# Causal masks of the row-major scores: added by VectorE inside the maximum, one head at a time, in place of identity matmuls on TensorE

## The chip, the cores and the metric

The kernel runs on one core of a Trainium2 chip. The metric is the device time of one execution in microseconds, and the time of a kernel is the median of its runs. TensorE multiplies matrices into PSUM, VectorE, ScalarE and GpSimd work on tiles of 128 partitions, and SyncE issues most of the DMAs. The profile calls the engines PE (with PEld for its weight loads), DVE, ACT, POOL and SP.

## The reference

Two residual layers stand one behind the other: cross attention with 16 heads of 32 dimensions, and a mixture-of-experts feed-forward layer. The change lies in the attention. Cut to what matters:

```python
# x: (4, 1024, 512), ctx: (4, 1024, 512); 16 heads of hd = 32
xn = layernorm(x)
qh = heads(xn @ Wq.T); kh = heads(ctx @ Wk.T); vh = heads(ctx @ Wv.T + bv)
scores = einsum('bhsd,bhtd->bhst', qh, kh) / sqrt(hd)
mask = triu(ones((S, S), bool), k=0).at[0, 0].set(False)
scores = where(mask, -inf, scores)          # query s sees keys t < s; query 0 sees key 0
out = einsum('bhst,bhtd->bhsd', softmax(scores), vh)
x = x + merge(out) @ Wo.T + bo
x = x + ffn(layernorm(x))                   # 128 experts, each takes the best of 32 tokens
```

Masked scores must count neither in the maximum of a row nor in its sum.

## The kernel before

The attention is cut into 16 units: 4 batches times 4 groups of four heads (`R = 4`, 128 of the 512 hidden columns). Each unit computes its scores twice. First come the row-major scores (tile `sc`, queries on the partitions), from which only the maximum of every row is taken. Then come the key-major scores (tile `st`, keys on the partitions), from which a second small matmul takes the maxima away (line 473, `ones` by `mxT`), ScalarE takes the exponential (`pr`, line 481), GpSimd zeroes what the mask hides (line 484), and TensorE multiplies by the values (`av`, line 517). VectorE and GpSimd each add up half of the exponentials (`acc`, lines 500 to 504).

`score_piece(u, k)` makes one piece of row-major scores: 128 queries against at most 512 keys, four heads. A unit has twelve pieces. Query tiles 0 to 3 give one piece each (128, 256, 384 and 512 keys); tiles 4 to 7 give two each, a full one of 512 keys and one of 128, 256, 384 or 512. The last piece of each query tile ends on the diagonal (`diag`): 8 of 12. A piece fills two PSUM tiles of two banks, each with two heads. `key_block(u, k)` is its counterpart for `st`. Both draw from the same pool `ps_s` with three buffers, so that the four tiles of a step pass through three places: the second `st` tile of a step needs the first `sc` tile of that step to have been read by VectorE, and the next piece's first `sc` tile needs the second one.

In a diagonal piece the mask is one more matmul for each head: the identity in bf16 as weights, a 128x128 mask with 0 and -3.0e38 as the moving side, added onto the last 128 columns (lines 405 to 410). Then VectorE takes the maximum over both heads of a tile in one `tensor_reduce` with the sign turned (line 413, tile `nm`). `split_maxima` cuts the maxima into three bf16 parts (lines 426 to 433), which TensorE turns (line 439) for the subtraction in `key_block`.

The main loop runs unit by unit and step by step: the score piece `k` of unit `u + 1` beside the key block `k` of unit `u`. Between the two, and behind them, TensorE works on fill: projections `pk`, `pq`, `pv` of later units and output projections `po` of the batch before. The order on TensorE, VectorE, ScalarE and GpSimd is what the program writes out; nothing reorders it. Where fill goes is decided while the program is built, by a small plan: `now` is TensorE's clock in the plan, `dve` and `act` those of its readers, `scores_given` books what a piece costs TensorE and how long its reader takes, and `slot(..., until)` puts in fill until the plan says that the next two buffers are free. `beside(0.9)` puts small pieces of VectorE's own work in (layer norm, splits, the scaling `at` of finished rows) at a fixed rate. In `normalize`, `rd` holds the reciprocals of the row sums (line 549) and is written to DRAM by a DMA.

The names of the profile: `sc` line 401 the score matmuls, line 407 the mask matmuls, line 413 the maxima, `st` lines 467 and 473, `xnT` lines 239 and 240 the layer norm of the turned input.

Of the kernel before, what the change touches and what calls it, by code (L numbers as in the profile page):

```python
# [11 lines left out]
F32 = mybir.dt.float32  # L12
BF16 = mybir.dt.bfloat16
AF = mybir.ActivationFunctionType
ALU = mybir.AluOpType
AX = mybir.AxisListType
PSUM = bass.MemoryType.PSUM

P = 128
EPS = 1e-5  # L20
NEG = -3.0e38
# [16 lines left out]
def attention_phase(  # L38
# [11 lines left out]
    nc = tc.nc  # L50
    ident, ident16, mhalf = consts
# [4 lines left out]
    R = P // HD  # L56
    HS = 512
# [5 lines left out]
    LARGE, SMALL, TURN = 0.86, 0.11, 0.2  # L63
    now, dve, act, bank = [0.0], [0.0], [0.0], [0.0]
# [3 lines left out]
    def given(engine, cost):  # L68
        engine[0] = max(engine[0], now[0] + 0.2) + cost
        return engine[0]  # L70

    def scores_free():
        return max(read[0], read[1]) + 0.1

    def scores_given(work, engine, cost):
        now[0] = max(now[0], scores_free()) + work
        for _ in range(2):
            read.popleft()
            read.append(given(engine, cost))
# [4 lines left out]
    wpool = units.enter_context(tc.tile_pool(name="attn_w", bufs=1))  # L84
# [5 lines left out]
    spool = units.enter_context(tc.tile_pool(name="attn_small", bufs=2))  # L90
# [27 lines left out]
    def later(name, cost, work, front=False):  # L118
        pieces_left[name] = (cost, work)
        if front:  # L120
            aside.appendleft(name)
        else:
            aside.append(name)
# [237 lines left out]

    masks = []
    for name, base in (("first", 0), ("strict", -1)):
        m = wpool.tile([P, P], BF16, tag=f"mask_{name}", name=f"mask_{name}")
        nc.gpsimd.memset(m, 0.0)
        nc.gpsimd.affine_select(
            out=m, in_=m, compare_op=ALU.is_ge, fill=NEG, base=base,
            pattern=[[-(P + 2), P]], channel_multiplier=P + 1,
        )
        masks.append(m)  # L370
# [8 lines left out]
    for n in range(2):  # L379
        m = wpool.tile([P, 4, R, HD], BF16, tag=f"mxs{n}", name=f"mxs{n}")  # L380
# [7 lines left out]
    def score_piece(u, k):  # L388
        i, c0, n = pieces[k]
        kT, qT = ks[u], qs[u]  # L390
        half = i // 4
        if (u, half) not in nms:
            nms[u, half] = spool.tile([P, 2, 4, R], F32, tag=f"nm{half}", name=f"nm_{u}_{half}")
        nm = nms[u, half]
        scs = [
            ps_s.tile([P, 2, HS], F32, tag="sc", name=f"sc_{u}_{k}_{g}") for g in range(2)
        ]
        diag = c0 + n == (i + 1) * P
        for r in range(R):
            rr = ds(r * HD, HD)  # L400
            nc.tensor.matmul(  # L401
                scs[r // 2][:, r % 2, :n], lhsT=qT[rr, ts(i, P)], rhs=kT[rr, ds(c0, n)],
                start=True, stop=not diag,
            )
        if diag:
            for r in range(R):
                nc.tensor.matmul(  # L407
                    scs[r // 2][:, r % 2, ds(n - P, P)], lhsT=ident16,
                    rhs=masks[0 if i == 0 else 1], start=False, stop=True,
                )  # L410
        scores_given(LARGE * n / HS + (0.45 if diag else 0.1), dve, 0.15 + 2.1e-3 * n)
        for g in range(2):
            nc.vector.tensor_reduce(  # L413
                nm[:, c0 // HS, i % 4, ts(g, 2)], scs[g][:, :, :n], AX.X, ALU.max, negate=True
            )

    def split_maxima(u, half):

# [112 lines left out]
    def normalize(u, h):  # L531

        def multiply(rows):
            if h == 0:
                atTs[u] = opool.tile([P, S], F32, tag="atT", name=f"atT_{u}", bufs=7)
            nc.vector.tensor_tensor(atTs[u][:, ts(h, HS)], avs.pop((u, h)), rows, ALU.mult)

        pd = ps_m.tile([P, P], F32, tag="pm", name=f"pd_{u}_{h}")  # L540
        for g in range(4):
            for r in range(R):
                nc.tensor.matmul(  # L543
                    pd[ds(r * HD, HD), :], lhsT=pick[:, g, :],
                    rhs=accs[u, h, r // 2][:, r % 2, ts(g, P)],
                    start=(g == 0), stop=(g == 3),
                )
        yield 0.9, dve, 1.0
        rd = spool.tile([P, P], F32, tag="rd", name=f"rd_{u}_{h}")
        nc.vector.reciprocal(rd, pd)  # L550
        if (u, h) != (NU - 1, 1):
            n = 2 * u + h
            nc.sync.dma_start(inverse_dram[ts(n, P), :], rd)
            rows = qpool.tile([P, 4, P], F32, tag="inverse", name=f"inverse_{u}_{h}", bufs=1)
            for r in range(R):
                nc.sync.dma_start(
                    rows[ds(r * HD, HD), :, :],
                    inverse_dram[ds(n * P + r * HD, 4), :].partition_broadcast(HD),
                )
            later(("at", u, h), 0.8, lambda: multiply(rows.rearrange("p g q -> p (g q)")), front=True)  # L560
            later(("wait", u, h), 0.9, lambda: None, front=True)
            return

        spread = ppool.tile([P, 2, HS], F32, tag="pr", name="spread")[:, 0].rearrange(
            "p (g c) -> p g c", g=4
        )
        for g in range(4):
            nc.vector.tensor_copy(
                spread[:, g, :].rearrange("p (r m) -> p r m", m=HD),
                ident.rearrange("p (r m) -> p r m", m=HD)[:, :, g : g + 1].to_broadcast(  # L570
                    [P, R, HD]
                ),
            )
        yield None
        pb = ps_m.tile([P, 4, P], F32, tag="pm", name=f"pb_{u}_{h}")
        for g in range(4):
            nc.tensor.matmul(pb[:, g, :], lhsT=spread[:, g, :], rhs=rd, start=True, stop=True)
        yield 4 * 2 * SMALL, dve, 0.7
        multiply(pb.rearrange("p g q -> p (g q)"))
# [5 lines left out]
    fill, soon, done = deque(), deque(), set()  # L585
# [106 lines left out]
    for u in range(-1, NU):  # L692
# [28 lines left out]
        for k in range(STEPS):  # L721
            if u + 1 < NU:
                if k in (0, 4):
                    ensure(("q", u + 1, k // 4), ("k", u + 1, k // 4))
                score_piece(u + 1, k)
                if k == 4:
                    split_maxima(u + 1, 0)
                if k == STEPS - 1:
                    split_maxima(u + 1, 1)
# [5 lines left out]
            if u >= 0:  # L735
                h, j = blocks[k]
# [9 lines left out]
            if u >= 0:  # L746

                def add_first(u=u, k=k):
                    add_sums(u, k, 0, nc.vector)

                def weigh(u=u, k=k):
                    h, j = blocks[k]
                    ensure(("v", u, j // 4))
                    weigh_values(u, k)
                    if j == 4 * (h + 1) - 1:
                        if h == 0 and NC <= u and u % NC == NC - 1:
                            ensure(("o", u // NC - 1, NT - 1))
                        soon.append((now[0], normalize(u, h)))

                add_sums(u, k, 1, nc.gpsimd)  # L760
                sums.append(add_first)
                pending.append(weigh)
# [332 lines left out]
def xattn_ffn(ctx: ExitStack, tc, x, xT, ctxT, wqT, wkT, wvT, bv, woT, bo, ctrl, f1, biasT, f2, tie, out):  # L1095
# [23 lines left out]
    with tc.manual_schedule(engines=engines):  # L1119
        attention_phase(  # L1120
            tc, consts, x, xT, ctxT, wqT, wkT, wvT, bv, woT, bo, ctrl, tie,
            x2_dram, stats_dram, inverse_dram, routed,
        )
# [39 lines left out]
```

## Time and profile before

| | us |
|---|---|
| Median of 3 runs | 1498.17 |
| Lowest, highest run | 1489.71, 1499.57 |
| The profiled execution, its own time | 1487.66 |
| Its span, first to last instruction | 1485.9 |
| Score pieces (line 401), first to last start | 39.9 to 1090.5 |
| Mask matmuls (line 407), first to last start | 40.4 to 1091.7 |
| Mean granted TensorE clock | 0.972 |

The profile is of one execution. A row of a group gives busy time, the mean duration of one instruction, and the idle time of its engine just before it with what ended it. Durations of matmuls overlap, because they are pipelined; the distance from start to start is what a matmul takes of TensorE's time. The attention with score pieces lies between about 40 and 1092 us; what follows is the end of the attention, the routing and the feed-forward layer.

### The profile page before, as it was taken

To read this page: it belongs to the slowest core of one execution; us is meant where nothing else is said; L and a number is where in the kernel's file an instruction comes from. 1 tells how busy PE (TensorE), PEld (TensorE's weight loads), DVE (VectorE), ACT (ScalarE), POOL (GpSimd) and SP (SyncE) were. 2 spreads that over 40 slices of the span, in tenths; PEclk is the share of its full clock that TensorE was granted. 3 is DMA by queue.
4 is the path that set the end of the run, shared out by engine and by line. 5 is a ranking of instruction groups with operands and counts; after the bars stand their busy time and mean duration, and the time that the engine had idled before them with its cause. 6 is when DMAs were issued, how large, how long until landed. Compare 5 with 4: busy or idle time off the path is not lost.

```text
span 1485.9 us, 31726 instructions
## 1 busy us (share of the span) xinstructions
PE 1400.1 (94%) x13704; PEld 739.5 (50%) x13704; DVE 926.8 (62%) x1377; ACT 502.7 (34%) x785; POOL 486.4 (33%) x557
## 2 busy tenths in 40 slices
PE   6999999999899999999999999999997988968996
PEld 4344544354344534443434344444533547868886
DVE  3666777565657676666767755655754554756664
ACT  1033333423232233232323233232333124636662
POOL 1034334343334343435253443434366200000212
PEclk9999999999999999999999999999997996988999
DMA  8011201002231300012211100010113788652654
GB/s 298 21 50 32 76 24 66 20 1 59 38 111 36 96 29 19 10 52 47 72 60 50 33 11 10 10 38 19 38 47 122 268 273 241 191 193 79 207 181 143
DMA packets 96972, 125.25 MB, mean 84 GB/s; under 512 B 12992, under 2 KB 54336, under 8 KB 96704
## 3 DMA queue, kind: packets, MB, share of 16 engines
q1 hardware_dynamic: 94272, 114.84, 24.9%
q0 software_dynamic: 2560, 8.39, 1.9%
q8 instruction: 107, 1.75, 0.5%
q14 instruction: 33, 0.27, 0.1%
HBM read 91.78 MB, written 31.42 MB: 83 GB/s over the span
## 4 chain that ended last, share of the span: by engine, by line
PE 78%; issue 7%; DVE 5%; DMA 5%; POOL 2%; ACT 1%; SPq 0%; POOLq 0%; DVEq 0%; ACTq 0%
PE sc L401 12%; PE st L467 10%; PE av L517 8%; PE pq L288 8%; PE pk L274 8%; PE pv L307 8%; PE po L348 5%; PE pd L957 3%; PE sc L407 3%; DVE nm L413 2%; PE pi L976 2%; PE st L473 2%; PE po L808 2%; PE pl L845 2%; PE pd L543 2%
## 5 line engine op out<-in xcount | busy, mean ns | idle before, releaser
L413 DVE TENSOR_REDUCE nm<-sc 128x2 f32<-128x1024 f32 (+3 forms) x384 | 349.1, 951 | 265.3 <-PE sc L407 178.9
L481 ACT ACTIVATE pr<-st 128x1024 f32<-128x1024 f32 (+3 forms) x384 | 290.4, 808 | 583.9 <-PE st L473 557.6
L484 POOL TENSOR_SCALAR_AFFINE_SELECT pr<-pr 128x256 f32<-128x256 f32 x256 | 122.5, 488 | 383.0 <-ACT pr L481 380.9
L504 POOL TENSOR_TENSOR acc<-acc,pr 128x1024 f32<-128x1024 f32 (+3 forms) x128 | 209.2, 1634 | 93.3 <-ACT pr L481 85.6
L401 PE MATMUL sc<-kT,qT 32*128 32x512 f32 (+3 forms) x1536 | 206.3, 531 | 8.6 <-ACT pr L481 4.9
L467 PE MATMUL st<-qT,kT 32*128 32x512 f32 (+3 forms) x1536 | 191.1, 534 | 4.6 <-DVE nm L413 4.5
L517 PE MATMUL av<-pr,v 128*32 128x512 f32 (+3 forms) x1536 | 166.2, 501 | 8.0 <-POOL pr L484 4.3
L274 PE MATMUL pk<-ct,w_k 128*128 128x512 f32 x256 | 131.0, 629 | 10.0 <-DMA w_k<-in_wkT_dram 9.2
L307 PEld LDWEIGHTS pv<-w_v,ct 128*128 128x128 f32 x1024 | 119.5, 192 | 34.6 <-issue 25.6
L504 DVE TENSOR_TENSOR acc<-acc,pr 128x1024 f32<-128x1024 f32 (+3 forms) x128 | 126.5, 989 | 9.2 <-POOL pr L484 9.0
L467 PEld LDWEIGHTS st<-qT,kT 32*128 32x128 f32 x1536 | 68.6, 183 | 127.5 <-issue 99.8
L401 PEld LDWEIGHTS sc<-kT,qT 32*128 32x128 f32 x1536 | 74.4, 183 | 115.4 <-issue 50.6
L307 PE MATMUL pv<-w_v,ct 128*128 128x128 f32 x1024 | 131.4, 281 | 0.2 <-DMA w_v<-in_wvT_dram 0.2
L288 PE MATMUL pq<-xnT,w_q 128*128 128x512 f32 x256 | 127.3, 616 | 1.5 <-ACT xnT L194 1.5
L501 POOL TENSOR_TENSOR acc<-pr,pr 128x768 f32<-128x768 f32 (+1 forms) x32 | 66.8, 2086 | 161.4 <-ACT pr L481 161.4
L1074 POOL DMA_DIRECT2D out_dram<-xr x32 | 24.2, 757 | 259.2 <-DVE xr L1073 258.8
L348 PE MATMUL po<-w_o,atT 128*128 128x512 f32 x192 | 95.5, 616 | 0.0
L517 PEld LDWEIGHTS av<-pr,v 128*32 128x32 f32 x1536 | 32.1, 108 | 94.9 <-issue 67.2
L274 PEld LDWEIGHTS pk<-ct,w_k 128*128 128x128 f32 x256 | 43.9, 194 | 69.0 <-issue 54.2
L473 PE MATMUL st<-mxT,ones 32*128 32x512 bf16 (+3 forms) x768 | 74.6, 322 | 0.3 <-DVE mxT L444 0.3
L288 PEld LDWEIGHTS pq<-xnT,w_q 128*128 128x128 f32 x256 | 43.0, 189 | 52.9 <-issue 46.2
L1058 PE MATMUL pt<-ident,y 128*128 128x128 f32 x512 | 58.3, 277 | 5.3 <-DVE y L1033 4.6
(101 smaller groups left out, 1495.2 us busy)
## 6 DMA issues: line engine op xcount, KB each, us to landing
ct<-in_ctxT_dram SPq DMA_DIRECT2D x8, 1024.0 KB, 5.1
xt<-in_x_dram SPq DMA_DIRECT2D x8, 1024.0 KB, 5.8
xr<-in_x_dram SPq DMA_DIRECT2D x32, 256.0 KB, 2.7
xn_dram<-x SPq DMA_DIRECT2D x8, 1024.0 KB, 4.8
xn<-xn_dram SPq DMA_DIRECT2D x8, 1024.0 KB, 5.8
f<-in_f_dram SPq DMA_DIRECT2D x16, 512.0 KB, 4.1
xr<-x_dram SPq DMA_DIRECT2D x32, 256.0 KB, 4.1
f<-in_f_dram SPq DMA_DIRECT2D x32, 256.0 KB, 4.3
```

Of the source, the lines that this page charges most:

```text
L274: nc.tensor.matmul(pk, lhsT=weights["k"][:, c, ts(hc, P)], rhs=cts[b, half][:, c, :], start=(c == 0), stop=(c == NC - 1),)
L288: nc.tensor.matmul(pq, lhsT=weights["q"][:, c, ts(hc, P)], rhs=xnTs[b][:, c, ts(half, HS)], start=(c == 0), stop=(c == NC - 1),)
L307: nc.tensor.matmul(pv[:, t, :], lhsT=cts[b, half][:, c, ts(t, P)], rhs=weights["v"][:, c, ts(hc, P)], start=(c == 0), stop=(c == NC - 1),)
L348: nc.tensor.matmul(po, lhsT=atTs[b * NC + c][:, ts(t, P)], rhs=weights["o"][:, c, :], start=(c == 0), stop=(c == NC - 1),)
L401: nc.tensor.matmul(scs[r // 2][:, r % 2, :n], lhsT=qT[rr, ts(i, P)], rhs=kT[rr, ds(c0, n)], start=True, stop=not diag,)
L413: nc.vector.tensor_reduce(nm[:, c0 // HS, i % 4, ts(g, 2)], scs[g][:, :, :n], AX.X, ALU.max, negate=True)
L467: nc.tensor.matmul(scs[r // 2][:, r % 2, :n], lhsT=kT[rr, ts(j, P)], rhs=qT[rr, ds(h * HS + q0, n)], start=True, stop=False,)
L473: nc.tensor.matmul(scs[r // 2][:, r % 2, :n], lhsT=ones16[rr, :], rhs=mxT[rr, ds(q0, n)], start=False, stop=True,)
L481: nc.scalar.activation(pr[:, :, :n], scs[g][:, :, :n], AF.Exp)
L484: nc.gpsimd.affine_select(out=d, in_=d, compare_op=ALU.is_ge, fill=0.0, base=0 if j == 0 else -1, pattern=[[0, 2], [P + 1, P]], channel_mu ...
L504: engine.tensor_tensor(acc, acc, pr[:, :, :n], ALU.add)
L517: nc.tensor.matmul(avs[u, h][rr, q0:], lhsT=vs[u][:, j, rr], rhs=pr[r // 2][:, r % 2, : HS - q0], start=(j == 0), stop=(j == last),)
```

## The change

The mask matmuls are gone. In diagonal pieces the two `tensor_reduce` are replaced by four `tensor_tensor_reduce`, one for each head: each adds the mask to the scores, multiplies by -1, writes the result back in place into PSUM, and gathers the minimum of the result in one element of `nm` (the same number as the turned maximum). Since the instruction runs over all `n` columns of a piece, the mask of diagonal pieces other than the first gets 512 columns, zero but for its last 128, of which the last `n` are used. Full pieces keep the `tensor_reduce`. In the program, one `tensor_tensor_reduce` is two instructions on VectorE: the main one, and one that writes the gathered value to `nm`. The plan's figures follow: a diagonal piece costs TensorE 0.1 in place of 0.45 beside its scores, and VectorE 0.5 in place of 0.15 beside 2.1e-3 for each column of a tile. `rd` gets one buffer in place of two.

```diff
     for name, base in (("first", 0), ("strict", -1)):
-        m = wpool.tile([P, P], BF16, tag=f"mask_{name}", name=f"mask_{name}")
+        width = HS if base else P
+        m = wpool.tile([P, width], BF16, tag=f"mask_{name}", name=f"mask_{name}")
         nc.gpsimd.memset(m, 0.0)
         nc.gpsimd.affine_select(
-            out=m, in_=m, compare_op=ALU.is_ge, fill=NEG, base=base,
+            out=m[:, width - P :], in_=m[:, width - P :], compare_op=ALU.is_ge, fill=NEG, base=base,
             pattern=[[-(P + 2), P]], channel_multiplier=P + 1,
         )
...
-                start=True, stop=not diag,
-            )
-        if diag:
-            for r in range(R):
-                nc.tensor.matmul(
-                    scs[r // 2][:, r % 2, ds(n - P, P)], lhsT=ident16,
-                    rhs=masks[0 if i == 0 else 1], start=False, stop=True,
+                start=True, stop=True,
+            )
+        scores_given(LARGE * n / HS + 0.1, dve, (0.5 if diag else 0.15) + 2.1e-3 * n)
+        for g in range(2):
+            if not diag:
+                nc.vector.tensor_reduce(
+                    nm[:, c0 // HS, i % 4, ts(g, 2)], scs[g][:, :, :n], AX.X, ALU.max, negate=True
                 )
-        scores_given(LARGE * n / HS + (0.45 if diag else 0.1), dve, 0.15 + 2.1e-3 * n)
-        for g in range(2):
-            nc.vector.tensor_reduce(
-                nm[:, c0 // HS, i % 4, ts(g, 2)], scs[g][:, :, :n], AX.X, ALU.max, negate=True
-            )
+                continue
+            for r in range(2):
+                sc = scs[g][:, r, :n]
+                nc.vector.tensor_tensor_reduce(
+                    sc, sc, masks[0] if i == 0 else masks[1][:, HS - n :],
+                    -1.0, 3.0e38, ALU.add, ALU.min,
+                    nm[:, c0 // HS, i % 4, ds(2 * g + r, 1)],
+                )
...
-        rd = spool.tile([P, P], F32, tag="rd", name=f"rd_{u}_{h}")
+        rd = spool.tile([P, P], F32, tag="rd", name=f"rd_{u}_{h}", bufs=1)
```

## The prediction, made before the changed kernel ran

> **What bounds the kernel now.** I read the page's first part, then busy time by stage, then the rows of VectorE by shape, the waits, and the order of time around mask matmuls.
>
> ```profile
> PE 1400.1 (94%) x13704; PEld 739.5 (50%) x13704; DVE 926.8 (62%) x1377; ACT 502.7 (34%) x785; POOL 486.4 (33%) x557
> ```
> ```profile
> 40.00:104.00 64.00, 62.29 (x439) 27.07 (x440) 42.15 (x72) 13.80 (x20) 9.72 (x14) 1.00 0.06 17
> 104.00:1040.00 936.00, 920.61 (x7384) 413.22 (x7382) 614.09 (x879) 291.11 (x406) 374.26 (x394) 1.00 0.14 41
> ```
>
> In the second fence a line is one stretch: busy us of PE, PEld, DVE, ACT and POOL, then the clock. From 104 to 1040 us, where nearly all score pieces lie, TensorE idles 15.4 of 936 us at full clock: it is the bound. VectorE is busy 66%. The change takes work from the full engine and gives more of it to one with a third of its time free.
>
> ```profile
> L413 DVE TENSOR_REDUCE nm<-sc 128x2 f32<-128x1024 f32 x192 | 225.8, 1217 | 141.2 <-PE sc L401 85.6 <-PE sc L407 55.0
> L413 DVE TENSOR_REDUCE nm<-sc 128x2 f32<-128x768 f32 x64 | 58.3, 952 | 45.6 <-PE sc L407 45.5
> L413 DVE TENSOR_REDUCE nm<-sc 128x2 f32<-128x512 f32 x64 | 41.2, 685 | 38.3 <-PE sc L407 38.3
> L413 DVE TENSOR_REDUCE nm<-sc 128x2 f32<-128x256 f32 x64 | 23.9, 415 | 40.1 <-PE sc L407 40.1
> L354 DVE TENSOR_TENSOR xr<-po,xr 128x512 f32<-128x512 f32 x24 | 16.5, 686 | 21.7 <-PE po L348 13.1 <-POOL acc L500 6.3 <-issue 2.1
> L337 DVE BATCH_NORM_AGGREGATE moments<-row_stats 128x2 f32<-128x6 f32 x32 | 5.8, 182 | 1.1
> ```
>
> The four first rows are the maxima to be replaced in diagonal pieces: about 0.15 us and 1.04 ns for each element of a partition. The fifth is the nearest row to the new instruction (two inputs, one in PSUM): 512 elements in 0.686 us, the same slope and start. The sixth stands for a very small instruction.
>
> ```profile
> DVE nm L413 <- PE sc L407: 178.9, 105, 5.9
> ...
> DVE nm L413 <- PE sc L401: 85.6, 44, 3.9
> ...
> PEld st L467 <- DVE nm L413: 9.1, 8, 5.1
> ```
>
> Waits (total us, times, longest): of 192 pairs of maxima 149 found VectorE idle, 1.8 us on average. TensorE hardly waits for maxima.
>
> ```profile
> 536.85 1.14 PE L401 MATMUL sc<-kT,qT 32*128 32x512 f32 x8
> 537.92 1.98 PE L348 MATMUL po<-w_o,atT 128*128 128x512 f32 x4
> 539.84 0.71 PE L467 MATMUL st<-qT,kT 32*128 32x256 f32 x8
> ...
> 542.64 1.14 PE L401 MATMUL sc<-kT,qT 32*128 32x512 f32 x8
> 543.72 0.40 PE L407 MATMUL sc<-mask_strict,ident 128*128 128x128 bf16 x4
> 543.95 1.94 PE L274 MATMUL pk<-ct,w_k 128*128 128x512 f32 x4
> 545.82 0.50 PE L467 MATMUL st<-qT,kT 32*128 32x128 f32 x8
> ```
>
> The same piece without and with masks (start, duration, both us). Without: 1.07 us to the fill, whose four matmuls take 1.92 to the next start. With: 1.08 us to the masks, 0.23 more to the fill, whose four take 1.87.
>
> **The change part by part.** *Mask matmuls, removed.* 16 units x 8 diagonal pieces x 4 heads = 512 matmuls with their weight loads. From start to start a group of four costs 0.23 - 0.05 = about 0.19 us, so 128 x 0.19 = 25 us of TensorE. The chain of waits books 0.33 us for such a group (its share, 3%, is about 42 us): it counts pipeline ends that the next matmul would have had anyway. [...] I take the measured distance, 25 us, and keep 42 as the upper end. All of it lies on TensorE, thus on the path, unless a wait opens in its place.
>
> *Maxima of diagonal pieces, replaced.* 256 `tensor_reduce` go, 512 `tensor_tensor_reduce` come, each of two instructions. Two reductions in a row take 2 x 1.217 - 0.08 = 2.35 us at 512 keys (a pair in the timeline), so a piece of n keys costs 0.22 + 4.18e-3 n now. The main new instruction is 0.15 + 1.045e-3 n from the fifth row. The write-out is in no row: its lower bound is nothing, with the overlap of neighbours kept (-0.08 each); its upper is the smallest instruction, 0.18, and 0.04 for the wait that the second of each pair now has on VectorE itself (neighbours that wait are that far apart in the timeline). I take 0.08 in sum, since the write-out is a single element with no input stream. A diagonal piece then costs VectorE 0.92 + 4.18e-3 n, 0.70 us more than before, whatever n; bounds +0.07 and +1.27. For 128 pieces: +90 us (9 to 163). VectorE was busy 699 us between 40 and 1100; it would be 789 of about 1035, 76% (83% at the upper end). It writes PSUM here, which no row of this trace does; nothing excludes that this is slower, and the second rival prices it.
>
> [...]
>
> *What covers it.* The second `st` tile waits for the first `sc` tile. From the scores of two heads (0.53 us, at 512) TensorE has the other two heads (0.53), fill (1.0 to 1.4 us in the built order) and the first `st` tile (0.53): 2.1 us and more. Two new instructions need 2 x 0.77 = 1.5 us at 512, against 1.2 plus a wait on half the masks. So the margin hardly moves, and only a VectorE that comes late breaks it. In the built order the plan has moved fill to where it helps: between scores and key block of pieces 0, 3 and 7 0.2 us more on average, behind the key block 0.1 to 0.3 us less. Where is VectorE late? In the normalization of a new batch:
>
> ```profile
> 440.00:460.00 20.00, 19.58 (x144) 9.47 (x144) 17.92 (x19) 6.40 (x7) 9.63 (x6) 1.00 0.07 15
> ...
> 520.00:540.00 20.00, 20.00 (x104) 6.79 (x100) 17.28 (x17) 5.98 (x7) 10.75 (x9) 1.00 0.08 27
> ```
>
> Two more stretches are like this (720: 17.84, 800: 17.14). Each holds about 2.7 diagonal pieces, +1.9 us, which fills VectorE to 19 to 20 of 20 us. I book 1 us of TensorE waiting in each, 4 us, and 3 us for the rest: 7.
>
> *Waits added.* The second instruction of a pair waits for the first (counted). Queued behind it are the sums `acc` and the splits; `acc` frees `pr` buffers for ScalarE, but those are six, three steps deep. The reciprocal now also waits for the previous `rd` to have been stored; they come about 24 us apart (560.45 and 584.73) and the slowest store in the trace took 11.4: nothing.
>
> *Moved.* SP keeps its 286 DMAs; a few context loads, row stores and residual loads change places with neighbours, as do projection evictions on ACT and residual additions on POOL. One such collision is in the trace: at 370 us VectorE waited 7.6 us for `inverse` behind large loads, TensorE then 4.3 us for `nm`, and the clock was 0.50 from 374 to 380 us, about 3 us more. It can go or come once more: -8 to +8, booked as 0. The wider mask is a longer memset of GpSimd before 40 us, hidden behind the first loads: 0 (uncovered, below 1 us).
>
> *Sum.* 25 - 7 = 18 us less than 1487.66, so 1470. The median of the runs is 10.5 us above the profiled execution: 1480.
>
> **The rivals.** *First: nothing moves.* The mask matmuls were covering VectorE, and TensorE now waits in their place; or the write-out costs the upper bound. For it: the plan puts fill only up to the moment that buffers are free, and the steps with little fill (pieces 1 and 5, 0.2 us) have nothing to put in. Against: 1.8 us of idle VectorE before three of four pairs. At +1.27 us a piece the four full stretches overflow by about 2 us each and smaller ones follow: 20 to 30 us of waiting against 25. Time 1490 to 1505.
>
> *Second: VectorE becomes the bound, slower.* If adding in place in PSUM runs at half rate (2.09 ns an element), a diagonal piece costs 1.0 + 8.4e-3 n: 2.1, 3.2, 4.2 and 5.3 us for 0.75, 1.3, 1.8 and 2.35. That is 17 us a unit, 273 in all, and VectorE stands at 94%. [...] The first four steps of a unit then need 22 us of VectorE in 20.5 (+2 x 16), the stretches of normalization overflow by 3 (x 8), and the first pair of each of the four larger pieces misses the 2.1 us margin by 0.5 (x 64): 88 - 25 = 63 us slower, 1560. It decides from the point where a piece costs about 1.3 us more than before.
>
> **How the numbers follow.** A measurement of this kernel can tell about 1% (15 us) from no change. Forecast as worked out: 0.41; its own range 1464 to 1492, and a quarter of it within 1%. First rival: 0.23. VectorE as the bound, in a milder or full form (1514 to 1620): 0.36, that high because the engine that takes the work gets nearly four times what the other gives, and its two prices are unmeasured. Faster 0.32, same 0.32, slower 0.36. The range that leaves out the lowest 0.05 and the upper part of the second rival is 1464 to 1545.
>
> **What would show it.** Right: no mask rows; `sc` followed by fill at 1.07 us; the new rows near 0.69 us at 512 and 0.29 at 128, with write-outs below 0.1; VectorE near 790 us up to the end of the score pieces; TensorE's waits for `nm` under 20 us. Wrong: main rows above 1 us at 512; waits of `st` or `sc` for `nm` of 40 us or more; clock below 1.00 in several stretches of the attention.

## The result, and the profile after

| | before | after |
|---|---|---|
| Median of 4 runs, us | 1493.95 | 1510.19 |
| Lowest, highest run, us | 1489.71, 1499.57 | 1508.08, 1513.26 |
| Profiled execution, us | 1487.66 | 1508.76 |
| Last score matmul starts at, us (profiled execution) | 1091.0 | 1116.0 |

The ratio is 1.0106, with a 95% interval of 1.0062 to 1.0149: the kernel became 1.1% slower, 16 us where 18 fewer were forecast. What follows that last score matmul takes nearly the same time in both (394.9 and 391.1 us of the profiled executions).

First the page's busy times and the first two stretches of the attention (busy us of PE, PEld, DVE, ACT, POOL, then the clock):

```profile
PE 1398.2 (93%) x13192; PEld 719.4 (48%) x13192; DVE 989.9 (66%) x2145; ACT 503.0 (33%) x785; POOL 491.2 (33%) x557
```
```profile
40.00:104.00 64.00, 60.96 (x321) 26.50 (x324) 45.23 (x133) 9.35 (x15) 8.30 (x13) 0.89 0.02 8
104.00:1040.00 936.00, 901.62 (x6888) 391.43 (x6876) 657.36 (x1511) 289.62 (x401) 368.53 (x381) 0.98 0.14 42
```

512 matmuls and as many weight loads are gone, and VectorE has 768 instructions more. But TensorE idles 34.4 us of the 936 where it idled 15.4, and its clock, 1.00 in both stretches before, is now 0.89 and 0.98. The new rows of VectorE (line 415 of the changed kernel, busy us and mean ns; line 409 keeps the maxima of full pieces; READ_ACCUMULATOR is the write-out):

```profile
L415 DVE CUSTOM_DVE_ANT_0 sc<-sc,mask_strict 128x512 f32<-128x512 f32 x128 | 87.8, 706 | 35.3 <-PE sc L402 32.9
...
L415 DVE DVE_READ_ACCUMULATOR2_ANT nm<- 128x1 f32 x512 | 72.1, 141 | 0.0
...
L415 DVE CUSTOM_DVE_ANT_0 sc<-sc,mask_strict 128x128 f32<-128x128 f32 x64 | 18.3, 307 | 30.6 <-PE sc L402 29.6
```

The main one runs at 1.04 ns an element ((706 - 307) / 384), in place in PSUM too. What four heads of a 512-key piece take shows in the order of time, first the two reductions of before, then the new instructions:

```profile
544.04 2.35 DVE L413 TENSOR_REDUCE nm<-sc 128x2 f32<-128x1024 f32 x2 [1.31 <-PE sc L407]
```
```profile
552.97 0.70 DVE L415 CUSTOM_DVE_ANT_0 sc<-sc,mask_strict 128x512 f32<-128x512 f32 x1 [1.15 <-PE sc L402]
553.58 0.14 DVE L415 DVE_READ_ACCUMULATOR2_ANT nm<- 128x1 f32 x1
553.76 0.70 DVE L415 CUSTOM_DVE_ANT_0 sc<-sc,mask_strict 128x512 f32<-128x512 f32 x1
554.37 0.14 DVE L415 DVE_READ_ACCUMULATOR2_ANT nm<- 128x1 f32 x1
554.37 0.73 DVE L415 CUSTOM_DVE_ANT_0 sc<-sc,mask_strict 128x512 f32<-128x512 f32 x1
...
555.81 0.69 DVE L508 TENSOR_TENSOR acc<-acc,pr 128x512 f32<-128x512 f32 x1
```

A write-out begins while the main instruction still runs. The second head of a tile starts 0.04 us after the write-out of the first has ended (0.79 us from main to main); the head behind that starts together with the write-out (0.61). From 552.97 to 555.81 are 2.84 us, against 2.35 for two reductions. TensorE's waits for maxima between 40 and 1110 us (total, times, longest):

```profile
PEld st L471 <- DVE nm L409: 17.0, 6, 6.8
PEld sc L402 <- DVE nm L415: 16.0, 20, 1.2
PE st L471 <- DVE nm L409: 12.8, 4, 6.0
PEld st L471 <- DVE nm L415: 12.5, 17, 1.3
...
PEld sc L402 <- DVE nm L409: 6.3, 10, 1.3
...
PE sc L402 <- DVE nm L415: 5.6, 7, 1.0
```

Weight loads waited 51.8 us for `nm`, against 22.8 before. Of those 22.8 the prediction shows the 9.1 of `st`; the larger part was this one:

```profile
PEld sc L401 <- DVE nm L413: 13.7, 24, 1.3
```

It is the next piece's first `sc` tile that waits for the second one to be read. The weight load's wait and that of the matmul behind it overlap (at 674.40 us of after one stall ends both, 6.78 and 5.95 us), so the two kinds are not added.

To see where the time is, I cut the attention into stretches of 2 us, from 40 us to the last score piece, and summed TensorE's idle time and what a busy TensorE lost to a granted clock below 1. The rest is work, with the waits that modelled matmul ends cover:

| kernel | last score | idle | lost to the clock | rest |
|---|---|---|---|---|
| before | 1091.0 | 18.0 | 2.7 | 1030 |
| after | 1116.0 | 39.1 | 22.4 | 1015 |

The masks' removal is there: 15 us less in the rest. It is more than paid back by 21 us more of idling and 20 us more lost at half clock, so that the last score comes 25 us later. Before had one drop of the clock (374 to 381 us); after has eight, of 3.4 to 10 us each, from 60, 74, 115, 231, 381, 671, 702 and 805 us on. Two of them show the two kinds. The first, after short waits (start, duration):

```profile
58.38 0.70 PE L402 MATMUL sc<-kT,qT 32*128 32x256 f32 x4 [0.35 <-DVE nm L409]
59.51 3.33 PE L402 MATMUL sc<-kT,qT 32*128 32x512 f32 x8 [0.43 <-DVE nm L409]
62.77 3.78 PE L274 MATMUL pk<-ct,w_k 128*128 128x512 f32 x4
...
67.73 1.98 PE L274 MATMUL pk<-ct,w_k 128*128 128x512 f32 x4
```

Two gaps of 0.4 us, then a clock of 0.50 from 60.49 to 67.31 us: the four `pk` matmuls that take 1.98 at 67.73 take 3.78 at 62.77. The second kind is the stall that before had once, at 370 us, and after has twice. SP's queue around 655 us, first before, then after:

```profile
642.60 0.38 SPq L216 DMA_DIRECT2D stats_dram<-ln_both  x1
653.76 0.34 SPq L235 DMA_DIRECT2D both<-stats_dram  x1
654.15 1.83 SPq L553 DMA_DIRECT2D inverse_dram<-rd  x1
658.06 1.71 SPq L556 DMA_DIRECT2D inverse<-inverse_dram  x4
```
```profile
654.35 0.38 SPq L216 DMA_DIRECT2D stats_dram<-ln_both  x1
654.78 0.58 SPq L557 DMA_DIRECT2D inverse_dram<-rd  x1
666.04 0.34 SPq L235 DMA_DIRECT2D both<-stats_dram  x1
666.77 2.06 SPq L560 DMA_DIRECT2D inverse<-inverse_dram  x4
```
```profile
671.73 0.69 DVE L542 TENSOR_TENSOR atT<-raw,inverse 128x512 f32<-128x512 f32 x1 [8.91 <-DMA inverse<-inverse_dram]
...
673.16 2.32 DVE L409 TENSOR_REDUCE nm<-sc 128x2 f32<-128x1024 f32 x2
...
674.40 1.22 PE L471 MATMUL st<-qT,kT 32*128 32x512 f32 x2 [5.95 <-DVE nm L409]
```

Before, the reciprocals `rd` were issued after the statistics of a layer norm had landed, and were on their way back 3.9 us later. After, they are issued 0.4 us behind the statistics and return only 12 us later. VectorE waits 8.91 us at `at` with the maxima queued behind it; TensorE waits 5.95 us for those, and its clock is 0.50 from 671.48 to 681.72 us. Nothing of this touches a mask.

### The profile page after: what moved, and what is told of

Its sections match the earlier page's. It is cut to its first block, busy times and chain, and to the rows that moved or that the text cites. A ratio compares the mean times of both kernels' runs of the same rounds, so it can differ in the third digit from the quotient of the medians.

```text
span 1507.1 us, 31644 instructions
## 1 busy us (share of the span) xinstructions
PE 1398.2 (93%) x13192; PEld 719.4 (48%) x13192; DVE 989.9 (66%) x2145; ACT 503.0 (33%) x785; POOL 491.2 (33%) x557
## 4 chain that ended last, share of the span: by engine, by line
PE 72%; DVE 10%; issue 8%; DMA 5%; POOL 2%; ACT 2%; SPq 0%; POOLq 0%; DVEq 0%; ACTq 0%
PE sc L402 10%; PE st L471 10%; PE pk L274 8%; PE pq L288 8%; PE av L521 8%; PE pv L307 8%; PE po L348 5%; PE pd L961 3%; PE pi L980 2%; DVE sc L415 2%; PE po L812 2%; PE st L477 2%; DMA inverse_dram<-rd 2%; PE pl L849 2%; PE pd L547 1%
## 5 line engine op out<-in xcount | busy, mean ns | idle before, releaser
L415 DVE CUSTOM_DVE_ANT_0 sc<-sc,mask_strict 128x256 f32<-128x256 f32 (+3 forms) x448 | 230.6, 535 | 154.6 <-PE sc L402 146.7
L508 POOL TENSOR_TENSOR acc<-acc,pr 128x1024 f32<-128x1024 f32 (+3 forms) x128 | 213.0, 1664 | 89.0 <-ACT pr L485 70.6
L471 PE MATMUL st<-qT,kT 32*128 32x512 f32 (+3 forms) x1536 | 208.4, 542 | 15.6 <-DVE nm L409 12.8
L409 DVE TENSOR_REDUCE nm<-sc 128x2 f32<-128x1024 f32 x128 | 150.5, 1216 | 59.1 <-PE sc L402 58.0
L274 PE MATMUL pk<-ct,w_k 128*128 128x512 f32 x256 | 135.0, 649 | 9.6 <-DMA w_k<-in_wkT_dram 9.2
L471 PEld LDWEIGHTS st<-qT,kT 32*128 32x128 f32 x1536 | 71.8, 185 | 150.6 <-issue 93.4
L508 DVE TENSOR_TENSOR acc<-acc,pr 128x1024 f32<-128x1024 f32 (+3 forms) x128 | 130.2, 1017 | 11.7 <-POOL pr L488 11.5
L307 PE MATMUL pv<-w_v,ct 128*128 128x128 f32 x1024 | 134.9, 286 | 1.4 <-ACT qT L293 1.4
L348 PE MATMUL po<-w_o,atT 128*128 128x512 f32 x192 | 98.6, 632 | 0.0
L477 PE MATMUL st<-mxT,ones 32*128 32x512 bf16 (+3 forms) x768 | 79.6, 326 | 0.0
```

The costliest lines, as they stand in the source:

```text
L274: nc.tensor.matmul(pk, lhsT=weights["k"][:, c, ts(hc, P)], rhs=cts[b, half][:, c, :], start=(c == 0), stop=(c == NC - 1),)
L307: nc.tensor.matmul(pv[:, t, :], lhsT=cts[b, half][:, c, ts(t, P)], rhs=weights["v"][:, c, ts(hc, P)], start=(c == 0), stop=(c == NC - 1),)
L348: nc.tensor.matmul(po, lhsT=atTs[b * NC + c][:, ts(t, P)], rhs=weights["o"][:, c, :], start=(c == 0), stop=(c == NC - 1),)
L409: nc.vector.tensor_reduce(nm[:, c0 // HS, i % 4, ts(g, 2)], scs[g][:, :, :n], AX.X, ALU.max, negate=True)
L415: nc.vector.tensor_tensor_reduce(sc, sc, masks[0] if i == 0 else masks[1][:, HS - n :], -1.0, 3.0e38, ALU.add, ALU.min, nm[:, c0 // HS, i ...
L471: nc.tensor.matmul(scs[r // 2][:, r % 2, :n], lhsT=kT[rr, ts(j, P)], rhs=qT[rr, ds(h * HS + q0, n)], start=True, stop=False,)
```

## The experiments

A time is the median of 4 to 20 runs; a ratio is to before on the same chip (there 1494.6 to 1495.6), with its 95% interval.

**e1: the change, but with the plan's figures of before.**

```diff
-        scores_given(LARGE * n / HS + 0.1, dve, (0.5 if diag else 0.15) + 2.1e-3 * n)
+        scores_given(LARGE * n / HS + (0.45 if diag else 0.1), dve, 0.15 + 2.1e-3 * n)
```

> The changed kernel with the plan's two figures of before (0.45 and 0.15 for a diagonal piece), so that fill, projections and DMAs stand in the order of before; only the masks' place differs. Theory A (VectorE comes late: the new instructions are longer and TensorE stands, whatever the order): 1505 to 1515 us, waits of TensorE for nm 20 us or more, several drops of the granted clock. Theory B (the new figures made a worse order, above all the row statistics' store ahead of the store of rd on SP at 650 us, which holds the multiplications of at): 1470 to 1485 us, no stall of 6 us near 650 to 690, waits for nm under 10 us.

1492.61 us, 0.9988 (0.9970 to 1.0007): no difference from before. The plan's figures alone are worth the 17.6 us between this run and after.

**e2: the reverse, before with the new figures.**

```diff
-        scores_given(LARGE * n / HS + (0.45 if diag else 0.1), dve, 0.15 + 2.1e-3 * n)
+        scores_given(LARGE * n / HS + 0.1, dve, (0.5 if diag else 0.15) + 2.1e-3 * n)
```

> The kernel before, masks by TensorE and one reduction for two heads, with the plan's new figures (0.1 and 0.5). Theory A: the order is harmless where VectorE is quick, 1488 to 1500 us. Theory B: most of the loss is here already, 1505 to 1525 us, with the stall at 650 to 690 us in the trace.

1515.55 us, 1.0130 (1.0091 to 1.0170). With the masks on TensorE the new figures cost 20 us; they need none of the change's instructions to do so.

**e3: no mask at all in the maxima, figures of before.** The row-major scores give nothing but the row's maximum, and softmax may subtract any number near it: here the maximum over the hidden scores of the piece too, which this kernel's maxima no longer leave out. All pieces use `tensor_reduce`; the mask matmuls and the new instructions are both gone, and what hides scores from the sums (line 484 of the kernel before) stays. The edit, against before:

```diff
-                start=True, stop=not diag,
-            )
-        if diag:
-            for r in range(R):
-                nc.tensor.matmul(
-                    scs[r // 2][:, r % 2, ds(n - P, P)], lhsT=ident16,
-                    rhs=masks[0 if i == 0 else 1], start=False, stop=True,
-                )
+                start=True, stop=True,
+            )
```

> The kernel before without its mask matmuls and with nothing in their place: the maximum of a row is taken over the hidden scores of its piece too, which softmax allows as long as nothing overflows; the order of before. It measures what 512 mask matmuls are worth when VectorE is given no more work. Both theories: 25 us less than before (0.19 us a piece), 1465 to 1475; if the chain's 0.33 us is right, 1450 to 1460; if masks only filled TensorE's waits, 1485 to 1495.

1467.67 us, 0.9815 (0.9773 to 0.9857). Against before, it is what the mask matmuls are worth: 27.4 us (21 to 34 by the interval). Against e1, it is what VectorE's new instructions cost in the same order of work: 24.9 us. (e1 also has `rd` with one buffer and the wider mask; in its trace no `rd` waits for a store.) The weight loads' waits for maxima, first of e1, then of e3:

```profile
PEld sc L402 <- DVE nm L415: 19.8, 29, 1.2
...
PEld st L471 <- DVE nm L415: 14.7, 20, 1.1
...
PEld st L471 <- DVE nm L409: 13.1, 10, 6.3
...
PEld sc L402 <- DVE nm L409: 6.0, 8, 1.3
```
```profile
PEld st L461 <- DVE nm L407: 14.1, 19, 5.7
PEld sc L401 <- DVE nm L407: 11.5, 20, 1.3
```

53.6 us against 25.6. Of e1's, 34.5 us are 49 waits for the new instruction, 0.7 us each, none long enough to stand out. `sc` and `st` share the growth: `sc` waits 25.8 us in place of 11.5, `st` 27.8 in place of 14.1.

**e4: the masks on both engines, each adding half, figures of before.**

The changed kernel with the mask matmuls of before put back beside the new instruction. The edit, against after (the plan's line is that of e1):

```diff
-NEG = -3.0e38
+NEG = -1.5e38
...
-                start=True, stop=True,
-            )
...
+                start=True, stop=not diag,
+            )
+        if diag:
+            for r in range(R):
+                nc.tensor.matmul(
+                    scs[r // 2][:, r % 2, ds(n - P, P)], lhsT=ident16,
+                    rhs=masks[0] if i == 0 else masks[1][:, HS - P :], start=False, stop=True,
+                )
```

> Masks added twice, by TensorE and by VectorE (each with half of the number), in the order of before: VectorE's new work alone, with nothing taken from TensorE. Theory A: 1515 to 1535 us, as TensorE keeps its masks and waits on top. Theory B: VectorE's extra 0.5 us a piece lies in idle time, 1490 to 1505 us.

1511.71 us, 1.0109 (1.0076 to 1.0142). Each engine has its price beside the other: VectorE's part costs 16.6 us over before, TensorE's 19.1 over e1. That is 8.3 us less for each than without the other (24.9 and 27.4), as much as the intervals of the four medians leave open (about 8 us, an estimate from the three ratios). That the two hide a part of each other is possible, and not shown.

The table of the attention, for these:

| kernel | last score | idle | lost to the clock | rest |
|---|---|---|---|---|
| e3, no masks | 1072.7 | 20.7 | 4.3 | 1008 |
| e1, VectorE, old figures | 1095.9 | 29.7 | 7.0 | 1019 |
| after, VectorE, new figures | 1116.0 | 39.1 | 22.4 | 1015 |
| e2, TensorE, new figures | 1123.5 | 30.2 | 19.9 | 1033 |
| e4, both, old figures | 1121.3 | 27.2 | 11.5 | 1043 |

With mask matmuls the rest is 1030 to 1043, without them 1008 to 1019. The new figures bring 15 us more at half clock with VectorE's masks (e1 to after) and 17 with TensorE's (before to e2).

Each row is one profiled execution, and these scatter: e1's is the second fastest of 20 (1487.64 us at a mean clock of 0.973; the others reach 1501.29 at 0.959), e2's the slowest of 5. Over all runs, the span times what the mean granted clock lacks to 1 averages 46 to 48 us for before, 50 for e1, 49 for e5, 52 for e6, 55 for e11, 59 for e2 and 62 for after. From e1 to after that is 12 of 17.6 us, from before to e2 14 of 20.5: the clock is about two thirds of it.

**e5, e6: one of the two figures at a time.** The change with only TensorE's new figure, 0.1 (e5), and with only VectorE's, 0.5 (e6).

```diff
+        scores_given(LARGE * n / HS + 0.1, dve, 0.15 + 2.1e-3 * n)
```
```diff
+        scores_given(LARGE * n / HS + (0.45 if diag else 0.1), dve, (0.5 if diag else 0.15) + 2.1e-3 * n)
```

> The changed kernel with only TensorE's new figure in the plan (0.1 for a diagonal piece; VectorE's stays 0.15). If the poor order comes from the TensorE figure, 1505 to 1515 us; if from the VectorE figure, 1485 to 1497 us with a mean clock of 0.97; if the two figures only shuffle an order that is as good as chance makes it, anything between, and the clock's drops in places of their own.

> The changed kernel with only VectorE's new figure in the plan (0.5 for a diagonal piece; TensorE's stays 0.45). If the poor order comes from the VectorE figure, 1505 to 1515 us; if from TensorE's, 1485 to 1497 us.

1491.84 us, 0.9981 (0.9955 to 1.0006), and 1492.10 us, 0.9978 (0.9960 to 0.9996). With VectorE's masks neither figure is slow by itself; both together are. Both of these have the second stall as well. In e6:

```profile
645.07 0.38 SPq L216 DMA_DIRECT2D stats_dram<-ln_both  x1
645.51 0.57 SPq L557 DMA_DIRECT2D inverse_dram<-rd  x1
...
658.15 1.85 SPq L560 DMA_DIRECT2D inverse<-inverse_dram  x4
...
662.85 0.69 DVE L542 TENSOR_TENSOR atT<-raw,inverse 128x512 f32<-128x512 f32 x1 [9.31 <-DMA inverse<-inverse_dram]
```

So the stall that after has over before does not make the difference by itself (e5 has it too, with `rd` issued 0.4 us behind the statistics at 650.57 us).

**e7, e8: the load of the statistics put later.** I took the stall to be SP's order: `both` waits on SP for its statistics, and `inverse` behind it. In e7 (after) and e8 (e3) the load is handed to the list of small pieces, 0.9 us of the plan later, with a small memset of VectorE on its tile.

```diff
-        spread_stats(0)
+        later(("hold", b), 0.9, lambda: None)
+        later(("spread", b), 0.0, lambda: spread_stats(0))
```

> The changed kernel with one thing moved: the load of both (the row statistics spread over the partitions) waits on SP until VectorE has come one step further, by a write of four columns, so that the loads of inverse no longer stand behind a load that waits for the store of the statistics. If those two stalls (near 380 and 670 us: 4.9 and 6.0 us of TensorE's waiting and some 4 us each at half clock) are a large part of the loss, 1488 to 1497 us and no wait for inverse above 4 us; if the loss lies in VectorE's lateness, 1503 to 1512.

> No masks in the maxima (as in the run without masks) and the same later load of both. The stall near 368 us in that run was 4.9 us of waiting and about 4 us at half clock: 1456 to 1463 us if it goes, 1466 to 1470 if another wait takes its place.

1514.81 us, 1.0124 (1.0070 to 1.0178), and 1466.27 us, 0.9807 (0.9754 to 0.9860). Nothing was won: that reading fell. SP's queue in e7, and the store's line in its chain of waits:

```profile
366.18 0.38 SPq L216 DMA_DIRECT2D stats_dram<-ln_both  x1
366.61 0.99 SPq L560 DMA_DIRECT2D inverse_dram<-rd  x1
378.37 1.71 SPq L563 DMA_DIRECT2D inverse<-inverse_dram  x4
```
```profile
366.61 11.74 DMA inverse_dram<-rd
```

`both` is out of the way, and the store of `rd` still takes 11.74 us. It is late behind the store of the statistics, issued 0.4 us before it.

**e9, e10: that store on GpSimd's queue instead,** in after and in e3.

```diff
-                nc.sync.dma_start(
+                nc.gpsimd.dma_start(
                     stats_dram[2 * b + half].rearrange("s (i p) -> p s i", p=P), mv
```

> The changed kernel with the store of the row statistics (1024 elements of 4 bytes) issued by GpSimd, on its own queue, in place of SP's. In the traces the store of rd that SP issued 0.4 us behind it took 11.4 to 11.9 us to land, VectorE waited 8 to 9 us for inverse and TensorE 5 to 6 us for nm, at 380 and 670 us. If the queue is what holds rd, both stalls and their half clock go: 1488 to 1497 us, longest wait for inverse under 4 us. If the 16 engines hold it whatever the queue, 1505 to 1515 us.

> No masks in the maxima, the order of before, and the statistics' store on GpSimd's queue: the same test where only one such stall (at 367 us) is left. If the queue holds rd, 1456 to 1462 us; if not, 1465 to 1470; if GpSimd's own issue of 1024 pieces delays its sums, 1470 or more.

1520.53 us, 1.0161 (1.0127 to 1.0195), and 1470.90 us, 0.9829 (0.9793 to 0.9866). Not faster either. From the chain of waits of e9:

```profile
363.24 10.36 DMA stats_dram<-ln_both
...
373.99 4.76 DMA inverse_dram<-rd
```

The store of the statistics takes 10.36 us on this queue too. That of `rd` no longer lies behind it and takes 4.76; but SP issues it only at 373.99, behind the load of `both`, which had waited for those statistics. With e7 one of the two obstacles was removed and the other held; with e9 the reverse. Both at once I did not try, so what the stall costs in full stays open.

**e11: the change with the figure that was measured,** 0.35 for VectorE. 2.84 us for the four heads at 512 keys are 1.42 a tile, and 0.35 + 2.1e-3 x 512 = 1.43.

```diff
-        scores_given(LARGE * n / HS + 0.1, dve, (0.5 if diag else 0.15) + 2.1e-3 * n)
+        scores_given(LARGE * n / HS + 0.1, dve, (0.35 if diag else 0.15) + 2.1e-3 * n)
```

> The changed kernel with VectorE's figure in the plan as measured (a tile of a diagonal piece takes 1.42 us at 512 keys and 0.63 at 128: 0.35 and 2.1e-3 a column) in place of 0.5; TensorE's stays 0.1. If the loss is a plan that has VectorE too slow, 1485 to 1495 us; if any order is as good as another, up to 1512.

1498.87 us, 1.0005 (0.9982 to 1.0029): 11 us better than after, and no better than e1, e5 and e6, whose figures are wrong.

**e12: e3 with a plan that knows that no masks are left** (0.1 and 0.15).

```diff
-        scores_given(LARGE * n / HS + (0.45 if diag else 0.1), dve, 0.15 + 2.1e-3 * n)
+        scores_given(LARGE * n / HS + 0.1, dve, 0.15 + 2.1e-3 * n)
```

> No masks in the maxima, and the plan told so (0.1 and 0.15 for every piece). If a plan that knows its costs gives the better order, 1455 to 1464 us; if orders differ by chance, 1460 to 1485.

1476.62 us, 0.9866 (0.9836 to 0.9897): 9 us slower than e3, whose plan still books 0.35 us for masks that are not there. A truer plan is not a better order. And here TensorE's figure alone does cost something, as it did not in e5.

## Why the prediction was wrong, step by step

The sum was 25 - 7 + 0 = 18 us faster. By the medians, the same terms are: 27.4 faster without mask matmuls (before to e3), 24.9 slower with VectorE's additions (e3 to e1), 17.6 slower with the new order (e1 to after): 15.1 slower.

Two terms failed, by nearly the same amount: what moved (0 booked, 17.6 measured) and the waits (7 booked, 24.9 measured). The waits alone would have left about no change, as in e1; only with the moved work does the kernel become slower.

- *Moved, "-8 to +8, booked as 0": the step that turned the sign.* The new order costs 17.6 us with the masks on VectorE and 20.5 with them on TensorE. I had looked for one stall that could come or go once more. It did come once more, but e5 and e6 have it too and are not slow. Most of it is clock: in the profiles after's last score comes 20 us behind e1's, made up of 15 us at half clock (22.4 - 7.0), 9 more of idling and 5 less in the rest; over all runs it is 12 us of clock. The forecast named the clock as a sign of error and gave it no price. It held that the plan had moved fill to where it helps; the waits of weight loads for `nm` are 51.8 us in the new order and 53.6 in the old one.
- *Waits, 7 us: the other step that failed.* They measured 24.9 (in the profiles 9 of idling, 3 at half clock, 11 in the rest). I priced places where VectorE has no time left, four stretches of 20 us, and reckoned the margin for the second `st` tile alone. The next piece's `sc` also waits, and did so before (13.7 us): about half of the growth lies there. The waits came in small pieces everywhere: VectorE's longer chain from scores to maxima is on TensorE's path at many steps although VectorE idles over a quarter of the time (751 busy of 1070 us from 40 on, in after). "The margin hardly moves" was wrong: 0.5 us more for four heads was enough to double the waits in front of weight loads (25.6 us in e3, 53.6 in e1).
- *Mask matmuls, 25 us: right.* 27.4 measured (128 x 0.19 is 24.3, which was rounded up). Distance from start to start was the better measure; the chain's 42 us were too high.
- *Price of a diagonal piece on VectorE, 0.70 us: somewhat high.* It is 0.49 at 512 keys (2.84 against 2.35). The main row was right (706 ns for 0.69 us), the write-out overlaps more than I had assumed: at 553.58 us it begins 0.61 us after the start of a main one of 0.70. Up to the end of the score pieces VectorE was busy 62 us more than before (761 between 40 and 1120, 699 between 40 and 1100), which is 128 x 0.49; 90 more were forecast.
- *Eight instructions of VectorE for two, on an engine with time to spare:* they cost 24.9 us (e3 to e1). No run separates their number from the 0.49 us that they add to each piece.
- *`rd` with one buffer and the wider mask, 0:* they were not tried alone, and are part of the 24.9. Nothing speaks against it: `rd` never waits for a store in the traces of e1 and after, and the first scores start at 40.9 us in e1 and 40.6 in e3.
- *Second rival, in-place PSUM at half rate:* refuted, 1.04 ns an element.
- *First rival, "the mask matmuls were covering VectorE, and TensorE now waits in their place", 1490 to 1505:* this is what the change does when the order stays. e1 has 1492.61. Its waits of 20 to 30 us against 25 are what was measured, though the way there was not: the write-out is cheap, not dear, and the overflow of "about 2 us each" is 0.6 to 1.4 us by the prediction's own figures (2.7 x 1.27 on top of 17.1 to 17.9 of 20). It was outweighed by idle VectorE "before three of four pairs", an average that says nothing on the steps where the maximum is late.

Not settled is why both figures together make a poor order where each alone does not. The orders of e1, e5, e6 and e11 lie within 7 us of each other, with 7 to 18 us lost to the clock; after and e2 lose 20 to 22. That is a difference of degree, and a reason beyond where the gaps happen to fall, which the last section shows, was not found.

## What to carry to other kernels

A cost figure in a plan is part of a change: it reorders everything behind it. Here the new figures cost 17.6 us, where the new instructions in the old order made no difference (e1). So run the new instructions in the old order and the old instructions in the new one before judging either. Work moved to an engine with idle time was not free here: TensorE awaits its result, and it cost 24.9 us (e3 to e1). So count the steps at which the result is awaited, not the idle share of the engine that takes the work. And ask first whether the work is needed: the maximum needs no mask, and leaving it out (e3 and e8, 1466 to 1468 us, 1.9% below before) beats both ways of applying it, as long as hidden scores don't tower over the visible ones so far that the exponentials vanish.

## What was not expected of the hardware

The granted clock fell to 0.50 after gaps of TensorE far shorter than the stalls: two of 0.4 us at 58 to 60 us, one of 1.29 us at 114, one of 0.67 at 229, and it stayed there for 3.4 to 10 us. After's eight drops cost 22.4 us, 2.8 each on average. The two drops at the stalls (waits of 4.93 and 5.95 us) are 6.0 of the 22.4 us; before each of the other six no gap was longer than 1.68 us.

Not every short gap does it, and gaps that did it at one place did not at another. In after's trace all eight drops between 40 and 1090 us begin on one grid with steps of 3.41 us and last one to three steps: they begin at 60.49, 74.14 and 115.10 us and so on, the second 4 steps and the third 16 steps behind the first. The drops that stretches of 2 us show in the traces of e1 to e9 and e11 lie on such a grid too; e5's begin at 61.36, 75.00, 112.56, 378.80 and 668.92 us, the later ones 4, 15, 93 and 178 steps behind the first. After has the same two gaps of TensorE, 1.68 and 0.69 us, at 505 and at 801 us; here are the steps around them (busy us of PE, PEld, DVE, ACT and POOL, then the clock):

```profile
504.19:507.60 3.41, 1.73 (x5) 0.49 (x3) 2.94 (x6) 0.00 (x0) 0.00 (x0) 1.00 0.32 77
507.60:511.01 3.41, 2.72 (x22) 2.27 (x21) 0.00 (x0) 0.60 (x1) 0.00 (x0) 1.00 0.43 154
801.18:804.59 3.41, 1.44 (x4) 0.61 (x5) 1.50 (x4) 0.60 (x1) 0.00 (x0) 1.00 0.28 115
804.59:808.00 3.41, 3.41 (x18) 3.41 (x17) 0.00 (x0) 0.00 (x0) 0.00 (x0) 0.50 0.12 48
```

At 505 us the gaps lie in two steps, 1.68 and 0.69 us of idling, and the clock stays at 1.00. At 801 us one step holds 1.97 us of them, and the next runs at 0.50. Between 40 and 1090 us of before and after, all 4 steps at full clock with at least 1.75 us of idling were followed by half clock, 4 of 19 with 0.7 to 1.75 us, and 1 of 573 with less. So the sum of idling says little about the clock: e1 and e2 idle 29.7 and 30.2 us, and lose 7.0 and 19.9 us to it.

The store of the row statistics, 1024 elements of 4 bytes, took 10.8 us to land in the median of after's six on SP's queue and 10.4 us in that of e9's six on GpSimd's; those in the chains of waits lie between 9.68 us (e1) and 12.64 (e5). A store of `rd` that SP issued 0.4 to 0.7 us behind it took between 11.39 us (before) and 12.58 (e4), 11.74 and 11.94 in after, where such a store takes 1.5 us in the median of after's 31. Where SP issued it after the statistics had landed, its load was under way 3.6 us later in e1 (at 661.88 us) and 3.9 in before (654.15).
